# Sums over sought rows placed ahead of the last twelve tiles of a product

## The chip, the cores and the metric

The kernel runs on one NeuronCore of a Trainium2 chip. Five engines work on their own instruction streams and wait for one another only through semaphores: TensorE (PE, matmuls into PSUM; its weight loads are listed apart as PEld), VectorE (DVE), ScalarE (ACT), GpSimd (POOL) and SyncE (SP), which here only issues transfers. All transfers share 16 DMA engines; SP, ACT and POOL each have a queue into them. The metric is the device time of one execution in microseconds, and the kernel before takes 2162.47 us in the median of 6 runs (2161.07 to 2164.54).

## The reference

Three graph convolutions on 6250 nodes with 256 features and 200000 edges, sorted by their destination, and then a feed-forward layer on the half of the nodes with the highest weight:

```python
x = x + gnn(layernorm(x))                  # three of the following, relu after the first two
    # h = x @ W
    # agg = segment_sum(h[src] * dinv[src] * dinv[dst], dst) + own term;  agg + b
    # dinv = rsqrt(deg), deg = edges into the node, and one for itself
x = x + ffn(layernorm(x))
    # weights = x @ wr + br;  the top half less one are chosen
    # y = gelu(sel @ w1 + b1) @ w2 + b2, scaled by the weight, added at its place
```

The change is in the preparation for the first convolution: deg and dinv, the product of the normed x with W1, and the places in the sorted edge list at which each piece of work begins.

## The kernel before

The nodes are 49 tiles of 128 (`NT = 49`). Tiles 0 to 30, where most edges lead, are done by counts: a strip of a destination tile holds how many edges lead from each node to each of its 128 nodes, and the convolution is a dense product of strips with hl, the scaled x W1 of all nodes. The rest is done by messages: the rows of edges are gathered and added up. hl is 49 x 2 x 256 values in each partition: a value, and what rounding it left.

All engines but SP run in the order in which the program is written (the whole front is under a hand-made schedule), so the place of a call in the text is its place in each engine's queue.

**The front, in order.** x is loaded in 7 groups of 7 tiles (three buffers). For each group, `fetch_rows` gathers with 7 indirect DMAs (L340, POOL) one row of 200 destinations for each node of 7 tiles: the row in which the node's edges end. `spread_of` takes mean and variance (L361, DVE), `roots` and `scales` make of them the scale and offset of each row of x, and then for each tile:

- `normal(t)`: the normed tile c_z (L397, ACT), and its two transposes (L400, PE)
- `product(t - 1)`: the copy c_zt out of PSUM (L293, ACT), and four matmuls with W1 (L298, PE)
- `stored(t - 2)`: the copy of the product into raw (L409, ACT)
- `seek(t)`: how many destinations in the tile's row lie before the node's end (L349, DVE), into a column of c2

After the last tile come: spread (L438, DVE), upto (L441, DVE), the matmuls L443 and L444 (PE) that turn upto into first, the number of edges before each node (L447, DVE), and `begins`. There are 20 "columns", each a list of 128 places in the edge list from which 128 edges are read: columns 0 to 16 for the counts and 17 to 19 for the messages (`SD = 17`, `SC = 20`). `begins(a, b)` makes the places of columns a to b - 1: a matmul for each column (L456, PE; 128 x 128 weights, 8 columns moved, two instructions for a column), a sum on DVE (junk_s, L458), and three small operations for the whole call (L461 to L463), the last of which writes `at`. It is called for column 0, then dinv is made (deg, whole_deg, a root on ACT at L272, four refining operations on DVE), and then it is called for the 19 others. Four small checks follow ("fits": matmuls L473, c_over L475). They are the last readers of the front's buffers, whose space hl then takes.

**From there to the main loop.** `take(a)` gathers with two indirect DMAs (L764, POOL) the destinations and sources of column a's edges; two columns are under way at a time. `codes_of` makes codes of them (7 operations on DVE, or 3 for columns 17 to 19), `flipped` transposes them (L794, PE), and `column` copies them out of PSUM (L805 or L808 and L809, ACT). `send_x(i)` makes hl of 7 tiles of raw (L814 on ACT, L815 on DVE, seven of each, about 2.9 us) and sends them to `sent[0]` in HBM (L818, SP, 1792 KB), where the message gathers find them. `count_bank` fills a strip: one-hot rows of 12 groups of edges at a time (L669, DVE, made one batch ahead), matmuls of these (L689, PE), and a copy of each bank of PSUM into the strip (L705, ACT). The first strip, of tile 30, has 16 banks of two groups each. The order before is:

```python
    send_x(0); next_column(); flip(); next_step()
    send_x(1)
    next_column()
    for k, bank in enumerate(BANKS[first_tile]):
        s = count_bank(...)          # send_x(2), (3), (4), (5) after banks 1, 5, 9, 13
    counted(...)                     # the strip's diagonal on DVE, and its transfer
    send_x(6)
```

**The main loop** (layer 0) has 7 steps for each of the 31 tiles. A step casts a seventh of a strip into piece (L727 on ACT, in some steps L729 on DVE), does its 7 matmuls with hl (L735, PE), in the first five steps of a tile fills some banks of the next tile's strip (three a step for tile 29, of three groups each), and handles one more column: `flip()` for the last one read and `next_column()` for the one after, for as long as columns are wanted. From step 7 on it gathers messages (L600, POOL), four sets ahead; their sums (L632, PE) begin some steps later.

Of the kernel before, what the change touches and what calls it, by code (L numbers as in the profile page):

```python
# [9 lines left out]
FP = mybir.dt.float32  # L10
# [11 lines left out]
P = 128  # L22
# [85 lines left out]
def by_counts(  # L108
# [303 lines left out]

    for t in range(XG):
        spread_of(t)
    scaled = scales(0, *roots(0))
    for a in range(0, NT, XG):
# [5 lines left out]
        for t in range(a, a + XG):  # L422
            normal(t, *scaled)
            product(t - 1)
            stored(t - 2)
            seek(t, found[t - a])
            if t == a + 1 and a + 2 * XG < NT:
                xts[a + 2 * XG] = load_x(a + 2 * XG)
        if a + XG < NT:
            scaled = scales(a + XG, *root)  # L430
        if 0 < a <= 4 * XG:
            in_order(a // XG - 1)
    product(NT - 1)
    stored(NT - 2)
    stored(NT - 1)
# [12 lines left out]


    begin = f1p.tile([P, SC], FP, name="begin")  # L450

    def begins(a, b):
        for c in range(a, b):
            t0 = TILE0[c]
            ps_s = ps_f.tile([P, SPAN], FP, name="ps_f")
            nc.tensor.matmul(ps_s, spread[:, c * P : (c + 1) * P], first[:, t0 : t0 + SPAN], start=True, stop=True)  # L456
            junk = small.tile([P, SPAN], FP, name="junk_s")
            nc.vector.scalar_tensor_tensor(  # L458
                junk, ps_s, 1.0, plan_sb[:, 3:, c], op0=OP.mult, op1=OP.mult, accum_out=begin[:, c : c + 1]
            )  # L460
        nc.vector.tensor_add(begin[:, a:b], begin[:, a:b], plan_sb[:, 1, a:b])  # L461
        nc.vector.tensor_scalar(begin[:, a:b], begin[:, a:b], float(E), None, op0=OP.min)
        nc.vector.tensor_copy(at[:, a:b], begin[:, a:b])  # L463

    begins(0, 1)
    nc.vector.tensor_sub(deg, upto[:, 1:], first)
    whole_deg = f1p.tile([P, NT], FP, name="whole_deg")
    nc.vector.tensor_scalar(whole_deg, deg, 1.0, 1.0, op0=OP.add, op1=OP.max)
    rsqrt(dinv, whole_deg, NT)
    begins(1, SC)  # L470
    for i in range(len(WIDTHS)):
        ps_w = ps_f.tile([P, NT], FP, name="ps_f")
        nc.tensor.matmul(ps_w, fits_sb[:, i, :P], deg, start=True, stop=True)  # L473
        over = small.tile([P, NT], FP, name="c_over")
        nc.vector.tensor_tensor(over, ps_w, fits_sb[:, i, P:], op=OP.is_gt)  # L475
        nc.vector.tensor_reduce(bad[:, 2 + i : 3 + i], over, axis=AX.X, op=OP.add)
    front.close()
    gnn = ExitStack()
    hl_pool = gnn.enter_context(tc.tile_pool(name="gnn1", bufs=1, side="right"))

    hl = hl_pool.tile([P, NT, 2, D], FR, name="hl")


    lay = ExitStack()
    later = {}
    ps_a = lay.enter_context(tc.tile_pool(name="c_ps_a", bufs=2, space=PSUM))
# [23 lines left out]
    def finish():  # L510
        while behind:
            next_step()

# [245 lines left out]

    def take(a):  # L760
        got = {}
        for name in ("dst", "src"):
            got[name] = f3p.tile([P, P], I32, name=f"got_{name}")
            nc.gpsimd.indirect_dma_start(  # L764
                out=got[name], out_offset=None, in_=ends[name],
                in_offset=bass.IndirectOffsetOnAxis(ap=at[:, a : a + 1], axis=0),
            )
        return got

    def codes_of(a, got):  # L770
        base, width = plan_sb[:, 0, a : a + 1], plan_sb[:, 2, a : a + 1]
        both = f3p.tile([P, 2, P], FP, name="both", bufs=1)

        j1 = f3p.tile([P, P], FP, name="j1", bufs=1)
# [927 lines left out]
```

## Time and profile before

The profiled execution took 2166.06 us, its span is 2164.2 us (the rest lies around it).

| | us | place |
|---|---|---|
| loads and the first three groups | 0 to 56.9 | x, transfers of the edge list |
| the other groups, up to the last sought row | 56.9 to 88.9 | L349 ends at 88.9 |
| x's product ends | 97.2 | L298 |
| column 0's places, dinv | 97.9 to 101.1 | L456, L276 to L281 |
| the 19 other columns | 101.2 to 109.6 | L456 |
| fits | 108.6 to 111.3 | L473 to L476 |
| first hl to the first matmul of the main loop | 111.16 to 146.72 | L814 to L735 |
| layer 0 to 2, feed-forward | to 2164.2 | |

In the whole span PE is busy 89% of the time, DVE 63%, ACT 56%, POOL 59%. In the front these shares say little: which engine is waited for changes every few microseconds, and so the front is read by the chain of waits and by windows. A window's row gives busy time and number of instructions of PE, PEld, DVE, ACT and POOL, then the clock that TensorE was granted (1.00 is full speed), the share of the DMA engines and GB/s. A timeline row gives start, duration, engine, line and names, the number of instructions merged into it, and in brackets how long the engine had stood idle and what ended that.

### The profile page before, as it was taken

The numbers are of one execution on the slowest core, as the hardware profiler recorded it, in microseconds if no ns is written. First come the engines' busy times: TensorE is split into PE (matmuls) and PEld (weight loads), VectorE is DVE, ScalarE is ACT, GpSimd is POOL, SyncE is SP. The second block draws the span as 40 slices with busy tenths as digits, with TensorE's granted clock in tenths as the row PEclk, the third lists the DMA queues.
The fourth block names the chain that finished last, engine by engine and source line by source line (L and its number), as shares of the span: only waits on it lengthen the run. The fifth ranks groups of instructions, "written<-read, shape, count | busy, mean of one in ns | idle before, by whom it ended". The sixth has DMA issues, their size and how long they took to land.

```text
span 2164.2 us, 30448 instructions
## 1 busy us (share of the span) xinstructions
PE 1920.6 (89%) x9636; PEld 1468.0 (68%) x9636; DVE 1366.5 (63%) x3370; ACT 1209.0 (56%) x1986; POOL 1268.5 (59%) x1228
## 2 busy tenths in 40 slices
PE   4949999999989886799999999999999999928997
PEld 3726767677766665478888888767777777716665
DVE  6685555667667778365555555488888888862111
ACT  3777777766656642565555555576666666502111
POOL 5425776666766530377777777477777777602221
PEclk9959999999999999899999999999999999957999
DMA  7387787888877640787777777598888888612110
GB/s 204 96 291 221 234 261 237 259 247 245 261 226 211 198 132 24 233 267 224 215 215 214 212 213 217 155 298 254 257 251 262 255 256 257 206 58 61 59 47 18
DMA packets 229052, 435.60 MB, mean 201 GB/s; under 512 B 35358, under 2 KB 139092, under 8 KB 224881
## 3 DMA queue, kind: packets, MB, share of 16 engines
q0 software_dynamic: 92992, 205.70, 34.9%
q1 hardware_dynamic: 104357, 192.11, 27.6%
q10 hardware_dynamic: 31532, 35.75, 4.9%
q8 instruction: 78, 1.28, 0.2%
q14 instruction: 93, 0.76, 0.1%
HBM read 335.50 MB, written 99.61 MB: 201 GB/s over the span
## 4 chain that ended last, share of the span: by engine, by line
PE 60%; DVE 21%; DMA 8%; ACT 6%; issue 3%; POOL 1%; ACTq 0%; SPq 0%; DVEq 0%; POOLq 0%
PE c_pa L735 32%; PE ps_g L632 9%; PE c_ph L1135 4%; PE c_po L1143 4%; PE ps_b L689 4%; PE c_pt L298 4%; DVE half L624 3%; ACT strip L705 2%; DVE hot_l L669 2%; DVE hot_w L669 2%; DMA message<-sent 2%; DMA half<-sent,source 2%; DMA c_xt<-in_x 1%; DVE pick_sel L609 1%; ACT piece L727 1%
## 5 line engine op out<-in xcount | busy, mean ns | idle before, releaser
L735 PE MATMUL c_pa<-hl,piece 128*128 128x512 f32 x4557 | 1264.2, 409 | 28.2 <-DVE hl L952 15.2
L735 PEld LDWEIGHTS c_pa<-hl,piece 128*128 128x128 f32 x4557 | 831.7, 191 | 195.9 <-DVE hl L952 15.3
L600 POOL DMA_INDIRECT msg<-sent,source x718 | 731.2, 1018 | 357.3 <-issue 145.9
L600 POOL DMA_INDIRECT half<-sent,source x359 | 392.3, 1093 | 209.0 <-issue 73.5
L609 DVE TENSOR_TENSOR pick_sel<-up_h,local 128x256 fp32r<-128x256 f16 x540 | 227.3, 421 | 284.3 <-PE ps_g L632 282.8
L705 ACT ACTIVATE strip<-ps_b 128x441 f16<-128x441 f32 (+3 forms) x441 | 303.4, 754 | 149.6 <-PE ps_b L689 147.7
L632 PE MATMUL ps_g<-half,pick_sel 128*128 128x512 f32 x1077 | 347.6, 401 | 37.3 <-DVE half L624 30.9
L619 ACT ACTIVATE half<-msg 128x512 fp32r<-128x512 f32 x360 | 225.3, 626 | 231.8 <-PE ps_g L632 156.7
L727 ACT ACTIVATE piece<-whole 128x896 fp32r<-128x896 f16 x341 | 320.3, 942 | 55.0 <-PE c_pa L735 27.8
L624 DVE TENSOR_TENSOR half<-msg,half 128x512 fp32r<-128x512 f32 x360 | 248.2, 689 | 81.5 <-ACT half L619 79.2
L689 PE MATMUL ps_b<-hot_w,hot_l 128*128 128x98 f16 (+2 forms) x2171 | 212.9, 225 | 64.9 <-DVE hot_l L669 48.1
L632 PEld LDWEIGHTS ps_g<-half,pick_sel 128*128 128x128 f32 x1077 | 200.4, 189 | 98.0 <-DVE half L624 48.8
L689 PEld LDWEIGHTS <-hot_l 128*128 128x128 f16 x2171 | 136.7, 101 | 182.4 <-issue 112.5
L727 ACT ACTIVATE piece<-strip 128x896 fp32r<-128x896 f16 x159 | 150.8, 950 | 99.9 <-PE c_pa L735 89.2
L669 DVE TENSOR_TENSOR hot_w<-up_w,codes 128x1176 f16<-128x1176 f16 (+2 forms) x181 | 165.4, 914 | 43.7 <-PE ps_b L689 43.4
L669 DVE TENSOR_TENSOR hot_l<-up_l,codes 128x1536 f16<-128x1536 f16 x181 | 172.1, 951 | 0.0
L1139 ACT ACTIVATE ht<-c_ph,b_sb 128x512 f32<-128x512 f32 (+2 forms) x64 | 38.0, 594 | 188.7 <-PE c_ph L1135 188.7
L1151 POOL DMA_INDIRECT out<-o,pick x25 | 25.2, 1007 | 140.8 <-DVE o L1148 140.8
L1147 DVE TENSOR_TENSOR o<-c_po,b_sb 128x256 f32<-128x256 f32 x25 | 10.6, 424 | 149.2 <-PE c_po L1143 149.2
L298 PE MATMUL c_pt<-c_wg,c_zt 128*128 128x256 f32 x392 | 99.8, 379 | 0.5 <-ACT c_zt L293 0.5
L1135 PE MATMUL c_ph<-yt,w_sb 128*128 128x512 f32 (+2 forms) x256 | 91.1, 516 | 0.6 <-DVE yt L1130 0.6
L1143 PE MATMUL c_po<-w_sb,ht 128*128 128x256 f32 x400 | 88.9, 382 | 0.0
(218 smaller groups left out, 1546.8 us busy)
## 6 DMA issues: line engine op xcount, KB each, us to landing
whole<-counts SPq DMA_DIRECT2D x434, 224.0 KB
counts<-strip SPq DMA_DIRECT2D x31, 1568.0 KB
c_rows<-ys ACTq DMA_DIRECT2D x49, 256.5 KB
sent<-hl SPq DMA_DIRECT2D x7, 1792.0 KB
sent<-c_h ACTq DMA_DIRECT2D x98, 128.0 KB
message<-sent SPq DMA_DIRECT2D x98, 128.0 KB
msg<-sent,source POOLq DMA_INDIRECT x718
c_xt<-in_x SPq DMA_DIRECT2D x48, 128.0 KB
```

The source lines that it names most:

```text
L298: nc.tensor.matmul(pt[:, 1, :], zt[:, k, :], w_sb[:, k, :], start=(k == 0), stop=(k == KD - 1))
L600: nc.gpsimd.indirect_dma_start(out=out_j, out_offset=None, in_=sent[layer], in_offset=bass.IndirectOffsetOnAxis(ap=source[:, i : i + 1], a ...
L609: nc.vector.tensor_tensor(pick[:, :n], up_h[:, None, :].to_broadcast([P, n, P]), local[:, b * GB : b * GB + n, None].to_broadcast([P, n, P ...
L619: nc.scalar.activation(half[:, :n, 0, :], msg[:, :n], AF.Copy)
L624: nc.vector.tensor_sub(half[:, :n, 1, :], msg[:, :n], half[:, :n, 0, :].bitcast(FP))
L632: nc.tensor.matmul(open_sums[t], pick[:, j, :], half[:, j].rearrange("p two d -> p (two d)"), start=(k == 0), stop=False)
L669: nc.vector.tensor_tensor(rows_k[:, : n // 2, :cols, :], up[:, None, :cols, :].to_broadcast([P, n // 2, cols, 2]), code.rearrange("p (k tw ...
L689: nc.tensor.matmul(pb[:, at_c : at_c + NT * width], row_l[:, k // 2, :, k % 2], row_w[:, k // 2, : NT * width, k % 2], start=(c == 0), sto ...
L705: nc.scalar.activation(strip[:, :, d0 : d0 + n * width].rearrange("p h (a j) -> p a h j", j=width), pb[:, at_c : at_c + n * NT * width].re ...
L727: nc.scalar.activation(piece, counts_7, AF.Copy)
L735: nc.tensor.matmul(pa, piece[:, j, :], hl[:, q].rearrange("p two d -> p (two d)"), start=(i == sources[0] and j == 0), stop=(i == sources[ ...
L1135: nc.tensor.matmul(ph[:, : n * P], w1_sb[:, k, f * P : (f + 1) * P], yt[:, k, : n * P], start=(k == 0), stop=(k == KD - 1),)
```

## The change

The last twelve tiles of x's product (`PAUSE = NT - 12 = 37`, tiles 37 to 48) are taken out of the loop over groups, where only their rows are still sought. After the last row come spread, upto, first, column 0's places, column 0's two gathers, and dinv. Then the twelve tiles are done, and after each of them the places of two more columns (1 and 2 after the first, one alone after the tenth, none after the last two); after the sixth also column 0's codes on VectorE. Behind the last product come column 0's transposes, the fits, the gathers of columns 17 and 18, and column 0's copy. The sends of x are spread over the 16 banks of the first strip: send 0 ahead of bank 0, sends 1 to 6 ahead of banks 2, 4, 6, 9, 11 and 13, and none after the strip. Column 17 is no longer handled ahead of the main loop but in its first step, and each later column a step later than before. The functions `take`, `codes_of`, `flipped`, `column` and the small scheduler move up in the text unchanged.

```diff
+    PAUSE = NT - 12
+
+    def x_product(t):
+        normal(t, *scaled[t // XG])
+        product(t - 1)
+        stored(t - 2)
+
     for t in range(XG):
         spread_of(t)
-    scaled = scales(0, *roots(0))
+    scaled = {0: scales(0, *roots(0))}
...
         for t in range(a, a + XG):
-            normal(t, *scaled)
-            product(t - 1)
-            stored(t - 2)
+            if t < PAUSE:
+                x_product(t)
             seek(t, found[t - a])
...
         if a + XG < NT:
-            scaled = scales(a + XG, *root)
+            scaled[a // XG + 1] = scales(a + XG, *root)
         if 0 < a <= 4 * XG:
             in_order(a // XG - 1)
-    product(NT - 1)
-    stored(NT - 2)
-    stored(NT - 1)
...
     begins(0, 1)
+    early_column = take(0)
     nc.vector.tensor_sub(deg, upto[:, 1:], first)
...
     rsqrt(dinv, whole_deg, NT)
-    begins(1, SC)
+    step_c = 2
+    for k, t in enumerate(range(PAUSE, NT)):
+        x_product(t)
+        if 1 + k * step_c < SC:
+            begins(1 + k * step_c, min(SC, 1 + (k + 1) * step_c))
+        if k == 5:
+            early_both = codes_of(0, early_column)
+    assert 1 + (NT - PAUSE) * step_c >= SC
+    product(NT - 1)
+    stored(NT - 2)
+    stored(NT - 1)
+    flipped(0, early_both)
     for i in range(len(WIDTHS)):
...
     columns_by = [0] + list(range(SD, SC)) + list(range(1, SD))
-    taken = [(columns_by[0], take(columns_by[0])), (columns_by[1], take(columns_by[1]))]
-    last_take = 2
+    taken = [(a, take(a)) for a in columns_by[1:3]]
+    last_take = 3
...
     first_tile = TILES_BY[0]
-    send_x(0)
-    next_column()
-    flip()
     next_step()
-    send_x(1)
     strips[first_tile] = f3p.tile([P, NT, P], F16, name="strip", bufs=1)
-    next_column()
+    sends = NT // XG
+    n_banks = len(BANKS[first_tile])
     for k, bank in enumerate(BANKS[first_tile]):
+        for i in range(ceil(sends * k / n_banks), ceil(sends * (k + 1) / n_banks)):
+            send_x(i)
         s = count_bank(strips[first_tile], first_tile, bank, s)
-        if k % 4 == 1 and k // 4 + 2 < NT // XG:
-            send_x(k // 4 + 2)
     counted(strips[first_tile], first_tile)
-    for k in range(2 + (len(BANKS[first_tile]) + 2) // 4, NT // XG):
-        send_x(k)
     raws.close()
```

## The prediction

> **What bounds the kernel now.** The change touches only the start, up to the main loop's first steps, so I read the start alone. First the chain of waits, which says what the start is made of:
>
> ```profile
> 78.12 0.32 DVE c_bn L361
> 79.00 0.60 ACT c_z L397
> ...
> 95.44 1.73 PE ps_x L298 x8
> ...
> 101.25 7.50 PE ps_f L456 x34
> ...
> 111.16 0.52 ACT hl L814
> ```
>
> From 79.0 to 97.2 us the chain runs over the last 14 tiles of x's product (TensorE and ScalarE in lockstep, 16.5 us from the first c_z to the last c_zt, 1.18 us a tile), then a short serial piece, then the 19 column sums (L456), four fit sums (L473), and only then does ScalarE begin hl. Next VectorE's timeline, for the moment from which the sums could start:
>
> ```profile
> 88.49 0.42 DVE L349 TENSOR_SCALAR_CACHE_REDUCE junk_r<-row,after_f 128x200 bf16<-128x200 uint16 x1
> 88.84 1.55 DVE L438 TENSOR_SCALAR spread<-row_sb,node_f 128x2560 f32<-128x2560 f16 x1
> 90.31 0.21 DVE L441 SCALAR_TENSOR_TENSOR upto<-c,c 128x49 f32<-128x49 f32 x1
> 97.59 0.21 DVE L447 COPY first<-ps_f 128x49 f32<-128x49 f32 x1 [7.07 <-PE ps_f L444]
> ```
>
> The sought rows end at 88.9 because their gathers land then (VectorE waits for row in front of four of the last six); VectorE has upto at 90.5 and waits 7.07 us behind x's product. That wait is what the change takes away. ScalarE's timeline shows the second place:
>
> ```profile
> 117.32 0.38 ACT L805 ACTIVATE codes<-ps_b 128x256 f16<-128x256 f32 x1 [3.26 <-PE ps_b L794]
> 117.60 2.89 ACT L814 ACTIVATE hl<-raw,c_dinv 128x256 fp32r<-128x256 f32 x7
> 124.36 0.89 ACT L705 ACTIVATE strip<-ps_b 128x392 f16<-128x392 f32 x2 [3.87 <-PE ps_b L689]
> ```
>
> ScalarE idles 3.26 and 3.87 us for the first column's codes and the first one-hot rows; from 124.36 on it is full until the loop. Last the windows, cut where the granted clock can change (its changes here all lie on a grid of 3.41 us); after the bounds come TensorE, its weight loads, VectorE, ScalarE, GpSimd, then the clock:
>
> ```profile
> 45.97:49.39 3.42, 0.00 (x0) 0.00 (x0) 3.21 (x13) 0.00 (x0) 0.00 (x0) 1.00 0.67 203
> 49.39:52.80 3.41, 1.65 (x5) 1.47 (x6) 3.31 (x20) 2.00 (x6) 1.53 (x2) 0.50 0.81 203
> 52.80:56.21 3.41, 3.41 (x11) 2.66 (x11) 2.11 (x9) 1.63 (x5) 2.50 (x4) 0.50 0.55 176
> ...
> 104.00:107.41 3.41, 3.41 (x17) 3.41 (x17) 1.39 (x16) 0.00 (x0) 0.00 (x0) 0.50 0.00 0
> ...
> 820.80:824.21 3.41, 3.02 (x23) 2.19 (x22) 2.27 (x3) 0.61 (x1) 0.00 (x0) 0.50 0.00 0
> 824.21:827.62 3.41, 1.47 (x28) 1.17 (x26) 3.40 (x5) 0.00 (x0) 0.00 (x0) 1.00 0.00 0
> 1960.85:1964.26 3.41, 2.61 (x12) 2.42 (x12) 0.85 (x2) 0.55 (x2) 2.51 (x3) 0.50 0.76 203
> 1964.26:1967.68 3.42, 2.83 (x13) 2.42 (x13) 0.42 (x1) 0.55 (x2) 1.89 (x2) 0.50 0.74 211
> ```
>
> An idle window halves the clock for the next one. A full window of x's product (52.80) restores it, but a window of nothing but column sums (104.00), busy throughout, does not. So I count the time in which columns move: at half clock 0.213 us for a transpose and 0.427 for a product matmul (an x tile is 2 and 4 of them, 2.13 us, as 51.15 to 53.34 to 55.48 us in the timeline), but 0.013 for a column sum of 8 columns, though these start 0.213 apart for their weight loads. By that count 1960.85 (12 of 0.213 us) has 0.75 and stays half; 820.80 has 0.77 (three of 0.427, about seventeen of 0.082) and the clock returns. Downwards, windows with 0.38 or less lose it, 0.39 keeps it.
>
> **The change, part by part.** *Removed:* the 7.07 us wait. *Lost:* TensorE and ScalarE did some seven of the twelve tiles while rows were still coming and upto was made (1.18 us each). Now both stand idle from 82.0 (the end of tile 35's product) to 90.6: 8.6 us hold a whole idle window wherever the grid lies, so TensorE restarts at half clock.
>
> *Serial piece.* Before, from L443's start at 97.01 to at (99.03) 2.0 us; at half clock four loads and two columns cost some 0.6 more, so at is ready near 93.2. deg, whole_deg and the root take from 98.95 to 99.65 before, so 93.9; c_z then reaches TensorE 0.64 later: 94.5.
>
> *Twelve tiles and 19 columns on TensorE.* Two columns add four loads: at half clock 3.5 spacings of 0.213 = 0.75 us (a transpose's load is about half a column's: 183 against 288 ns), so a step is 2.88; at full clock loads start 0.11 apart (97.85 to 98.21), so 0.36 and a step 1.54. ScalarE needs 1.08 a tile, VectorE about 1.1 a step for two junk_s and three small operations: both are covered. codes_of(0) at step 5, seven operations of 2.0 us, is covered by VectorE's slack, and without it would cost up to 2. Moved time in a window of these steps: 0.65 to 0.80 of it, above 0.77 for more than half of the positions. I take a return of the clock 6.5 us after the start (one to two windows, 3.4 at best, 12 after three bad ones). Then 6.5/2.88 = 2.26 tiles are done at half clock; 9.74 x 1.18 + 7.25 x 0.36 = 14.1 us follow, 0.9 for the last product: 94.5 + 6.5 + 14.1 + 0.9 = 116.0. The flip of column 0 (0.25) and four fits with their c_over, 0.43 each on VectorE, end 2.0 later: hl starts at 118.0 against 111.16, **+6.8 us**. Each window of 3.41 us more at half clock costs 1.6.
>
> [...]
>
> *From hl to the loop.* Before: first c_pa 35.56 us after hl's start (111.16 to 146.72). Now the codes are there: after send 0 (2.9), VectorE's tail (0.5), one-hot rows (2.2) and the first sums (0.6) the first strip comes at 6.1 us, after one idle time of 3.2 instead of 3.26 + 3.87. That is 3.9 less on ScalarE, which then does the same 16 strips and 6 sends without a break; column 17's flip, 0.5 us of ScalarE, moves from the first loop step to a later one where it is covered by matmuls. Against it: the rows for the next tile (2.0 us, VectorE) now lie after the last send and ahead of the strip's diagonal, so c_pa itself starts only 3.1 earlier. Bounds 2.4 and 5.4 (7.1 if both idle times vanished); the first steps' chain runs over ScalarE's strips and pieces, so I take **-4.0**.
>
> *Queues.* SP: seven sends of 1792 KB, issued 114.65 to 145.99 before, now closer together; at some 380 GB/s each needs 4.8 us, and they end several us earlier after hl's start. Nothing is gained: the first message gather (162.30) follows directly on the column gathers of GpSimd's queue. GpSimd: column 0's two gathers (0.94 each) start near 93.5 and have 8 us to land; the later columns' come one step later, the last before step 7's messages, whose sums begin at 186 in the profile: some 13 us of cover for some 4 us. *Downstream* nothing else moves.
>
> Sum: +6.8 - 4.0 = +2.8 us. The profiled execution took 2166.06 us (span 2164.2), 3.6 above the median of 2162.47; I set the difference on the median: **2165.3**.
>
> **The rivals.** *1. The clock does not return among the columns.* For it: 0.75 was not enough, and 0.80 is my own count. Then 12 x 2.13 + 9 x 0.75 + 0.37 + 1.7 - 0.8 (a late return) = 33.6, hl at 94.5 + 33.6 + 2.0 = 130.1, +18.9 - 4.0 = +14.9: 2177.4. *2. Faster.* TensorE keeps full clock through the gap and both idle times of ScalarE vanish: start 93.7, 12 x 1.18 + 9.5 x 0.36 + 0.9 = 18.5, hl at 114.2, +3.0 - 7.7 = -4.7: 2157.8. It decides from where the second stage gives more than the first costs; the idle window at 45.97 speaks against the first half, the one-hot rows against the second. *3. The change does not overlap:* columns and product alternate with stalls through the two ps_f banks, 0.3 us a step, 10 steps: 2168.3. VectorE's slack speaks against it.
>
> **How the numbers follow.** Likeliest 0.60, rival 1 0.27, rival 2 0.06, rival 3 0.07. The likeliest one's own range: return at 3.4 us (-1.4) with -5.4, to 12 us (+2.6) with -2.4: 2162.5 to 2169.5. The whole range drops most of rival 2 and keeps rival 1: 2161.5 to 2178.5. About 0.2%, 4.3 us, is what a measurement can tell from no change: two thirds of the likeliest case (0.40) lie within it; its rest (0.20), rival 1 and rival 3 lie above (0.54), rival 2 below (0.06).
>
> **What would show it.** first (L447) near 91.5 with no wait on L444; no TensorE work from 82 to 90.6; half clock at 94.5, full from about 101; hl at 118; no wait of ScalarE for codes, one of about 3 us for the first strip; c_pa about 32 us after hl. A clock still half at 110 means rival 1; hl before 114 rival 2. I am wrong if the loop's first steps give back what ScalarE gained, or if the restart at half clock does not happen.

## The result and the profile after

The changed kernel takes 2171.59 us in the median of 25 runs (2161.96 to 2176.53), the kernel before beside it on the same chip 2162.78 us (50 runs): a ratio of 1.0034, 95% interval 1.0026 to 1.0042, or +7.4 us (5.6 to 9.1). A second comparison of the same pair gave 1.0022 (1.0010 to 1.0034), +4.8 us. The ratios are taken over all fast runs (one run of the kernel before, of 4855 us, is slow and left out) and not from the medians, which lie 8.8 and 2.9 us apart. The change makes the kernel slower, as forecast and by more than forecast. The profiled execution took 2170.12 us, its span is 2168.2 us; its sought rows end at 86.88 us instead of 88.92, a difference that no edit explains, so the stages below are counted from the end of the rows.

Line numbers have moved: spread is L441, upto L444, first L450, the column sums L537, a column's gathers L483 and its codes L494 to L506, hl L830 and L831, the strip's copies L773, its diagonal L789, piece L795 and L797, the loop's matmuls L803.

First TensorE's timeline of the changed kernel (start, duration, line, names; in brackets the idle time before and what ended it). It answers the wait of 7.07 us shown for before:

```profile
79.68 0.38 PE L298 MATMUL ps_x<-c_wg,c_zt 128*128 128x256 f32 x1
88.53 0.66 PE L446 MATMUL ps_f<-upto,up 128*128 128x49 f32 x2 [8.47 <-DVE upto L444]
...
92.46 0.69 PE L400 MATMUL ps_x<-c_ident,c_z 128*128 128x128 f32 x2 [1.94 <-ACT c_z L397]
95.36 0.67 PE L400 MATMUL ps_x<-c_ident,c_z 128*128 128x128 f32 x2
97.78 0.42 PE L400 MATMUL ps_x<-c_ident,c_z 128*128 128x128 f32 x2
99.27 0.42 PE L400 MATMUL ps_x<-c_ident,c_z 128*128 128x128 f32 x2
100.75 0.41 PE L400 MATMUL ps_x<-c_ident,c_z 128*128 128x128 f32 x2
```

The wait behind x's product is gone: TensorE now waits 8.47 us for upto. The first step of the twelve, transposes to transposes, takes 2.90 us; from 97.78 on a step takes 1.48 us. Two different speeds for the same work are the clock, which the windows show (us; busy time and number of PE, PEld, DVE, ACT, POOL; clock; DMA share; GB/s):

```profile
80.20:83.61 3.41, 0.00 (x0) 0.00 (x0) 1.63 (x9) 0.00 (x0) 2.52 (x3) 1.00 0.30 90
83.61:87.03 3.42, 0.00 (x0) 0.00 (x0) 1.44 (x7) 0.00 (x0) 0.95 (x1) 0.51 0.22 60
87.03:90.44 3.41, 1.61 (x6) 1.43 (x6) 1.65 (x4) 0.00 (x0) 0.00 (x0) 0.50 0.00 0
90.44:93.85 3.41, 1.47 (x6) 1.22 (x6) 2.24 (x12) 2.04 (x6) 1.88 (x2) 0.50 0.09 19
93.85:97.27 3.42, 3.42 (x13) 2.97 (x12) 0.85 (x7) 1.26 (x3) 0.00 (x0) 0.50 0.08 19
97.27:100.68 3.41, 3.41 (x26) 3.18 (x25) 1.69 (x14) 2.38 (x7) 0.00 (x0) 1.00 0.00 0
```

One idle window, 80.20 to 83.61, halves the clock from 83.6 on; the first full window of the steps, 93.85 to 97.27, brings it back. ScalarE's timeline shows the second stage:

```profile
113.47 0.38 ACT L524 ACTIVATE codes<-c_pt 128x256 f16<-128x256 f32 x1
114.94 2.90 ACT L830 ACTIVATE hl<-raw,c_dinv 128x256 fp32r<-128x256 f32 x7 [1.09 <-DVE c_over L569]
121.18 0.89 ACT L773 ACTIVATE strip<-ps_b 128x392 f16<-128x392 f32 x2 [3.34 <-PE ps_b L757]
121.95 2.90 ACT L830 ACTIVATE hl<-raw,c_dinv 128x256 fp32r<-128x256 f32 x7
```

The two idle times of before, 3.26 and 3.87 us, have become one of 3.34. The loop's first matmul starts at 146.42, 31.47 us after hl (35.56 before). Up to here the forecast holds. Then come the loop's first steps, for which it had expected no change; VectorE's timeline there:

```profile
159.16 0.23 DVE L501 TENSOR_SCALAR hi_i<-got_src 128x128 int32<-128x128 int32 x1 [1.27 <-DMA got_src<-src_p,at]
...
164.46 0.28 DVE L494 TENSOR_SCALAR j<-got_dst,plan_sb 128x128 f32<-128x128 int32 x1 [1.57 <-DMA got_dst<-dst_p,at]
164.92 0.23 DVE L501 TENSOR_SCALAR hi_i<-got_src 128x128 int32<-128x128 int32 x1 [0.17 <-DMA got_src<-src_p,at]
...
166.71 0.22 DVE L789 TENSOR_TENSOR strip<-strip,c_ident_h 128x128 f16<-128x128 f16 x1
166.84 0.62 DVE L797 CAST piece<-strip 128x896 fp32r<-128x896 f16 x1
```

VectorE does its work here in the order of the program: it waits for the gathered edges of columns 1 and 2, and behind these waits stand the strip's diagonal and a piece for the loop. TensorE's next matmuls wait for the diagonal:

```profile
166.93 0.41 PE L513 MATMUL ps_b<-c_ident,both 128*128 128x128 f32 x2 [2.34 <-DVE strip L789]
```

The chain of waits of this stretch agrees; its longest piece is that gather:

```profile
154.69 0.29 DVE j L494
...
156.50 8.33 DMA got_src<-src_p,at
...
166.24 0.24 DVE hi_i L505
```

So between loop steps 4 and 5 the changed kernel loses 2.9 us: counted from the first matmul of the loop, steps 4, 5 and 7 start after 15.17, 20.68 and 24.15 us, before after 15.62, 18.19 and 21.57.

### The profile page after: what moved, and what is told of

Its sections match the earlier page's. It is cut to its first block, busy times and chain, and to the rows that moved or that the text cites. A ratio compares the mean times of both kernels' runs of the same rounds, so it can differ in the third digit from the quotient of the medians.

```text
span 2168.2 us, 30475 instructions
## 1 busy us (share of the span) xinstructions
PE 1911.6 (88%) x9636; PEld 1459.6 (67%) x9636; DVE 1371.7 (63%) x3397; ACT 1210.3 (56%) x1986; POOL 1276.1 (59%) x1228
## 3 DMA queue, kind: packets, MB, share of 16 engines
q1 hardware_dynamic: 104357, 192.11, 27.5%
## 4 chain that ended last, share of the span: by engine, by line
PE 60%; DVE 21%; DMA 9%; ACT 5%; issue 3%; POOL 1%; ACTq 0%; SPq 0%; DVEq 0%; POOLq 0%
PE c_pa L803 33%; PE ps_g L700 9%; PE c_po L1154 4%; PE c_ph L1146 4%; PE ps_b L757 4%; PE c_pt L298 4%; DVE half L692 2%; DVE hot_w L737 2%; DVE hot_l L737 2%; DMA msg<-sent,source 2%; DMA c_xt<-in_x 2%; ACT strip L773 2%; DVE pick_sel L677 1%; DMA half<-sent,source 1%; DVE c_z L596 1%
## 5 line engine op out<-in xcount | busy, mean ns | idle before, releaser
L803 PE MATMUL c_pa<-hl,piece 128*128 128x512 f32 x4557 | 1263.4, 409 | 29.7 <-DVE hl L963 14.8
L803 PEld LDWEIGHTS c_pa<-hl,piece 128*128 128x128 f32 x4557 | 830.2, 191 | 198.9 <-DVE hl L963 17.7
L773 ACT ACTIVATE strip<-ps_b 128x441 f16<-128x441 f32 (+3 forms) x441 | 303.9, 754 | 146.2 <-PE ps_b L757 143.9
L795 ACT ACTIVATE piece<-whole 128x896 fp32r<-128x896 f16 x341 | 320.1, 942 | 59.2 <-PE c_pa L803 30.2
L795 ACT ACTIVATE piece<-strip 128x896 fp32r<-128x896 f16 x159 | 150.7, 950 | 99.5 <-PE c_pa L803 88.9
```

The costliest lines, as they stand in the source:

```text
L773: nc.scalar.activation(strip[:, :, d0 : d0 + n * width].rearrange("p h (a j) -> p a h j", j=width), pb[:, at_c : at_c + n * NT * width].re ...
L795: nc.scalar.activation(piece, counts_7, AF.Copy)
L803: nc.tensor.matmul(pa, piece[:, j, :], hl[:, q].rearrange("p two d -> p (two d)"), start=(i == sources[0] and j == 0), stop=(i == sources[ ...
```

## Where the time went, in all profiles

Each row is one profiled execution; the first column is counted from the end of the last sought row to the first hl, the second from there to the first matmul of the loop, the third from there to loop step 7. "Ahead" is the number of columns whose gathers are issued ahead of the loop. The kernels are explained below; the last two ran on a chip on which the kernel before, too, takes 2399 us.

| kernel | rows to hl | hl to loop | loop to step 7 | ahead | ratio to before |
|---|---|---|---|---|---|
| before | 22.2 | 35.6 | 21.6 | 4 | 1 |
| after | 28.1 | 31.5 | 24.2 | 3 | 1.0034 |
| after_again | 30.4 | 31.5 | 25.8 | 3 | 1.0022 |
| first_half | 27.9 | 32.0 | 21.5 | 4 | 1.0019 |
| second_half | 25.4 | 31.4 | 25.7 | 3 | 1.0018 |
| col17_ahead | 30.2 | 32.1 | 22.6 | 4 | 1.0023 |
| three_takes | 28.9 | 31.5 | 20.8 | 4 | 0.9999 |
| warm | 26.4 | 31.5 | 23.5 | 3 | 1.0003 |
| pause5 | 27.9 | 31.5 | 25.3 | 3 | 1.0014 |
| pause5_three | 27.6 | 31.5 | 20.6 | 4 | 0.9997 |
| pause5_three_warm | 21.5 | 31.5 | 20.6 | 4 | 0.9952 |
| late_sends | 28.3 | 31.5 | 23.8 | 3 | 1.0026 |
| before_extra | 27.5 | 35.6 | 21.5 | 4 | 0.9983 |
| after_extra | 29.0 | 31.5 | 25.5 | 3 | 0.9968 |

For the changed kernel the first profile gives +5.8 - 4.1 + 2.6 = +4.3 us, the second +8.2 - 4.1 + 4.2 = +8.3; the two measured differences are +7.4 and +4.8. The runs of one kernel on one chip scatter by 4 to 10 us to either side of their median, and some of that lies behind these stages: from step 7 to the end of the span it is 1997.6 us in the first profile of the changed kernel and 1991.4 in the second. So the sum of stages is good to a few microseconds and no more. The third column splits by the fourth without overlap: 20.6 to 22.6 us with four columns ahead, 23.5 to 25.8 with three.

The table below says why. It gives, for three columns, when their two gathers are issued and when VectorE first reads each of the two (columns are handled in the order 0, 17, 18, 19, 1, 2, and so on; times from the timelines of GpSimd and VectorE):

| column | issued before | read before | issued after | read after (wait) |
|---|---|---|---|---|
| 19 | 121.48, 122.72 | 150.35, 151.87 | 146.83, 148.08 | 154.69, 155.35 (0.38) |
| 1 | 147.09, 148.33 | 155.36, 155.56 | 150.24, 151.71 | 157.62, 159.16 (1.27) |
| 2 | 150.90, 152.37 | 159.26, 159.64 | 155.25, 156.50 | 164.46, 164.92 (1.57, 0.17) |

For column 2, GpSimd's issues and VectorE's first readers, before:

```profile
150.90 0.95 POOL L764 DMA_INDIRECT got_dst<-dst_p,at  x1 [1.63 <-DVE j L775]
152.37 0.94 POOL L764 DMA_INDIRECT got_src<-src_p,at  x1 [0.52 <-DVE both L778]
159.26 0.27 DVE L775 TENSOR_SCALAR j<-got_dst,plan_sb 128x128 f32<-128x128 int32 x1
159.64 0.23 DVE L782 TENSOR_SCALAR hi_i<-got_src 128x128 int32<-128x128 int32 x1
```

and its issues after (the readers are shown above, at 164.46 and 164.92):

```profile
155.25 0.95 POOL L483 DMA_INDIRECT got_dst<-dst_p,at  x1 [2.59 <-DVE j L494]
156.50 1.15 POOL L483 DMA_INDIRECT got_src<-src_p,at  x1 [0.30 <-issue]
```

Before, columns 0, 17, 18 and 19 are gathered ahead of the loop, and the loop's first steps handle 18, 19, 1 and 2. After, column 17 is one step later, the buffer of its gathers comes free one step later, and the loop's first steps must gather column 19 as well and handle five columns. Where VectorE waits, the time from issue to reading is the time that the gather takes, its landing and the signal of it included: 7.3 to 9.2 us, while the sends and the counts fill the DMA engines. Before, the two gathers of columns 1 and 2 are read 8.3 and 7.2 us after their issue, without a wait. After, VectorE stands in line for them after 7.4 to 7.6 us (157.62 - 150.24; it is done with the one-hot rows at 162.89, column 2's gather was issued at 155.25) and, for the second one, after 6.2 to 6.6: about 1 us sooner, and that is too soon.

## The experiments

The rival views were: the front alone costs the time and the rest is a gain; the waits in the loop are a chance of one execution; the gathers land late because of what fills the queue, or only when it is empty. The letters in the expectations name such views.

**col17_ahead**: the changed kernel, with column 17 handled ahead of the loop again, behind the sends of bank 0.

```diff
     for k, bank in enumerate(BANKS[first_tile]):
         for i in range(ceil(sends * k / n_banks), ceil(sends * (k + 1) / n_banks)):
             send_x(i)
+        if k == 0:
+            next_column()
```

> The changed kernel, with column 17 handled ahead of the first strip again (its codes after send 0, and the next gathers issued there), so that every later column comes in the step in which it came before the change. Theory A (a column a step later meets gathers that land late while the sends fill the DMA engines, and VectorE waits for it ahead of the strip's diagonal and the next piece): the 2.9 us that the changed kernel loses between its loop steps 4 and 5 (from -0.75 to +2.18 us against before) go, 0.6 us of VectorE ahead of the first one-hot rows come back: some 2.3 us less than the change, a ratio of 1.0024 instead of 1.0034. Theory B (all of the loss is the restart at half clock and the idle gap ahead of it, the loop only shifts noise): no difference from the change, 1.0034.

Measured: 2169.43 us against 2165.66, 1.0023 (1.0011 to 1.0035); the interval holds both figures. The loop's first steps came back to 22.6 us, but column 17's work now stands in ScalarE's stretch (hl to loop 32.1 instead of 31.5), and in the profiled execution the clock returned only 9.3 us after x's restart at 94.75. The repair works where it was aimed, and the total can't tell the two theories apart.

**three_takes**: the changed kernel, with a third pair of buffers for gathers, so that columns 17, 18 and 19 are gathered ahead of the loop.

```diff
-            got[name] = f3p.tile([P, P], I32, name=f"got_{name}")
+            got[name] = f3p.tile([P, P], I32, name=f"got_{name}", bufs=3)
...
-    taken = [(a, take(a)) for a in columns_by[1:3]]
-    last_take = 3
+    taken = [(a, take(a)) for a in columns_by[1:4]]
+    last_take = 4
```

> The changed kernel with three columns' gathers under way instead of two (three buffers each), the columns themselves in the order of the change. Theory A1 (the gathers of columns 1 and 2 land late, 8 to 9 us after issue, because sends fill the DMA engines): each gather is issued a loop step, some 3.5 us, earlier, so the wait of about 2.9 us at step 5 goes: 1.0021. Theory A2 (not the landing but the 2 us of codes on VectorE in step 4, in front of the diagonal): little changes, 1.0032 to 1.0036.

Measured: 2165.0 us, 0.9999 (0.9985 to 1.0013). Five columns are still handled in the first steps, but VectorE's timeline has no wait for them any more:

```profile
159.13 0.28 DVE L494 TENSOR_SCALAR j<-got_dst,plan_sb 128x128 f32<-128x128 int32 x1
159.32 0.22 DVE L501 TENSOR_SCALAR hi_i<-got_src 128x128 int32<-128x128 int32 x1
...
163.01 0.28 DVE L494 TENSOR_SCALAR j<-got_dst,plan_sb 128x128 f32<-128x128 int32 x1
163.21 0.22 DVE L501 TENSOR_SCALAR hi_i<-got_src 128x128 int32<-128x128 int32 x1
```

The first steps take 20.8 us, 0.8 less than before and 3.3 less than with the change. So it isn't the number of columns that costs the time, but the time from issue to need. The total lies 5 to 8 us below the changed kernel's two ratios, more than these 3.3 us and below both expected figures; what goes beyond the 3.3 us is not explained, and is within the scatter of the runs.

**warm**: the changed kernel, with idle matmuls on TensorE in the gap (nobody reads their result): 16 ahead of spread and 4 behind column 0's places.

```diff
+    def warm(n):
+        pt = ps_t.tile([P, 2, D], FP, name="c_pt")
+        for _ in range(n):
+            nc.tensor.matmul(pt[:, 1, :], ident, wg_sb[0][:, 0, :], start=True, stop=True)
+
+    warm(16)
...
     begins(0, 1)
+    warm(4)
```

> The changed kernel with 16 matmuls whose result nobody reads ahead of the matmuls that make first, and 4 more after column 0's sum, which keep TensorE moving through the time in which it idles. If the restart at half clock costs what the changed profile shows (from 92.46 to 97.30 us at half clock, 1.7 steps that take 2.5 us at full clock, and 0.6 us in the serial piece): 2.9 us less than the change, 1.0021. If the clock returns later in most executions than in the profiled one, more: up to 1.000. If the idle gap alone counts and not the clock: 1.0034.

Measured: 2167.1 us, 1.0003 (0.9987 to 1.0018). hl starts 26.4 us after the rows instead of 28.1, and the steps ran at full clock from 94.7 on, 0.2 us after the restart. So part of what the clock costs can be bought back: 1.7 us of hl's start in these two profiles, where 2.9 were expected. The total is lower than that accounts for, but its runs lie between 2156.69 and 2170.32 us.

**first_half**: the changed front with the order of before from hl on (send 0, send 1, one column, then the sends behind banks).

```diff
+    send_x(0)
+    send_x(1)
...
-    sends = NT // XG
-    n_banks = len(BANKS[first_tile])
+    next_column()
     for k, bank in enumerate(BANKS[first_tile]):
-        for i in range(ceil(sends * k / n_banks), ceil(sends * (k + 1) / n_banks)):
-            send_x(i)
         s = count_bank(strips[first_tile], first_tile, bank, s)
+        if k % 4 == 1 and k // 4 + 2 < NT // XG:
+            send_x(k // 4 + 2)
     counted(strips[first_tile], first_tile)
+    for k in range(2 + (len(BANKS[first_tile]) + 2) // 4, NT // XG):
+        send_x(k)
```

> The front of the change (sums ahead of the last twelve tiles, column 0's codes in their midst), but sends and column 17 in the order of before: sends 0 and 1 first, column 17's codes, then the strip with the others. First strip at 5.8 + 0.5 + 0.6 + 2.2 + 0.6 = 9.7 us after hl's start instead of 6.2, then 16 strips and 5 sends, so the first c_pa some 1.2 us later than in the change, and by theory A the 2.9 us of step 5 do not arise: 1.0026. By theory B it is 1.0040.

Measured: 2169.95 us, 1.0019 (1.0007 to 1.0031): the interval holds A's figure and not B's. One thing is worth keeping: hl to the loop is 32.0 us here, so 3.6 of the 4.1 us that the second stage gains come from the codes' being ready, and the spreading of the sends adds 0.5. And with column 17 ahead of the loop the first steps take 21.5 us, as before.

**second_half**: the front of before, column 0 made ahead of hl, and then the order of the change with its spread sends and column 17 in the loop.

```diff
     first_tile = TILES_BY[0]
-    send_x(0)
     next_column()
     flip()
     next_step()
-    send_x(1)
...
-    next_column()
...
+        for i in range(ceil(sends * k / n_banks), ceil(sends * (k + 1) / n_banks)):
+            send_x(i)
```

> The kernel before with only the second part of the change: its front as it was, then column 0's codes, flip and copy ahead of all sends, the sends spread over the banks as in the change, and column 17 a step later. hl starts some 3 us later (codes 2.0, flip 0.7, copy 0.4), the first c_pa 31.5 us after that: 0.9 us earlier than before. Theory A: step 5 then loses 2.9 us: +2.0 us, 1.0009. Theory B: -0.9 us, 0.9996.

Measured: 2167.34 us against 2162.97, 1.0018 (1.0003 to 1.0032), above both expectations, with A's figure inside the interval and B's outside. This half is no gain by itself: column 0 ahead of hl costs 3.1 us, hl to the loop gives 4.1, and the first steps lose 4.1 again, with the front of before. The loss in the loop belongs to the later columns, not to the change of the front.

**pause5** and **pause5_three**: five tiles instead of twelve are left behind the sums, with four columns a step, so that TensorE has no idle gap ahead of the sums; the second one with the third pair of buffers as well.

```diff
-    PAUSE = NT - 12
+    PAUSE = NT - 5
...
-    step_c = 2
+    step_c = 4
...
-        if k == 5:
+        if k == 3:
             early_both = codes_of(0, early_column)
```

> The changed kernel with the last five tiles after the sums instead of the last twelve (four columns after each tile, column 0's codes after the fourth). Seven tiles more are done while rows are still sought, which fills TensorE's idle 8.5 us almost up to upto. If the twelve tiles cost because seven of them had been free: x's part then takes 5 x 1.9 + 0.9 from about 94 us and, with a restart at half clock, 2.5 more; hl starts near 109 instead of 111.2, the second stage gives 4, the loop takes 2.9 back: -3.6 us, 0.9983. If the restart's cost were all: like the change, 1.0030.

> The same with three columns' gathers under way. Theory A1: 2.9 us less than with five tiles alone: -6.5 us, 0.9970. Theory A2: as that one, 0.9983.

Measured: 2167.18 us, 1.0014 (1.0000 to 1.0027), and 2163.76 us, 0.9997 (0.9984 to 1.0010). The third pair of buffers gives the loop's first steps 4.8 us (25.3 to 20.6), as A1 has it, but neither kernel is as fast as was expected. The gap was gone and the clock was still lost, and this time it didn't come back among the columns at all (half from 92.7 to 150.7 us, and from 92.3 to 150.3). The place is the short serial piece from first to c_z: in pause5_three's windows the stretch 88.91 to 92.33 holds 1.17 us of TensorE's work.

```profile
85.50:88.91 3.41, 3.32 (x19) 2.36 (x17) 2.14 (x7) 1.94 (x6) 0.00 (x0) 1.00 0.04 13
88.91:92.33 3.42, 1.17 (x8) 0.89 (x8) 2.08 (x12) 1.30 (x5) 1.10 (x2) 0.99 0.01 2
92.33:95.74 3.41, 3.41 (x14) 3.05 (x14) 1.06 (x10) 1.60 (x4) 0.78 (x1) 0.50 0.13 38
95.74:99.15 3.41, 3.41 (x15) 3.05 (x14) 1.03 (x9) 1.25 (x3) 0.00 (x0) 0.50 0.00 0
```

With four columns a step TensorE is busy throughout, and yet the clock stays at half: much of it is column sums, which move eight columns each (how much, is counted in the last section).

**after_again**: the changed kernel once more, for a second profile.

> The changed kernel once more, unaltered, beside the next kernels on their chip, and with a second profile. Both theories of the loop's first steps (A: VectorE waits in its queue for the gathers of column 2, which land 8 to 9 us after their issue while the sends fill the DMA engines; B: the waits of the first profile were a chance of that one execution) expect a ratio of 1.002 to 1.004. A expects in the second profile again a wait of more than 1 us of VectorE for got_src or got_dst between 158 and 166 us, and 2 to 3.5 us lost between the starts of loop steps 4 and 5 beside the kernel before; B expects neither.

Measured: 2170.11 us against 2167.23, 1.0022 (1.0010 to 1.0034). The waits are there again, in VectorE's timeline:

```profile
163.14 0.23 DVE L501 TENSOR_SCALAR hi_i<-got_src 128x128 int32<-128x128 int32 x1 [1.17 <-DMA got_src<-src_p,at]
...
167.99 0.29 DVE L494 TENSOR_SCALAR j<-got_dst,plan_sb 128x128 f32<-128x128 int32 x1 [1.12 <-DMA got_dst<-dst_p,at]
168.97 0.23 DVE L501 TENSOR_SCALAR hi_i<-got_src 128x128 int32<-128x128 int32 x1 [0.69 <-DMA got_src<-src_p,at]
```

Steps 4 and 5 start 15.1 and 20.7 us after the loop's start, as in the first profile: no chance. The clock was different. x restarts at 94.21, and the windows show three at half clock, the one of the restart included, before it returns at 103.8:

```profile
93.56:96.97 3.41, 2.76 (x10) 2.40 (x11) 1.39 (x7) 2.22 (x8) 1.64 (x2) 0.50 0.15 38
96.97:100.39 3.42, 3.42 (x14) 3.06 (x14) 1.11 (x12) 1.79 (x5) 0.00 (x0) 0.50 0.00 0
100.39:103.80 3.41, 3.41 (x14) 2.96 (x13) 1.31 (x10) 1.42 (x5) 0.00 (x0) 0.50 0.00 0
103.80:107.21 3.41, 3.41 (x24) 3.15 (x23) 1.70 (x15) 2.44 (x7) 0.00 (x0) 1.00 0.00 0
```

So the clock returns 9.6 us after the restart instead of 4.8, and hl starts 2.3 us later after the rows (1.6 for each window was the forecast's price). The kernel is the same; what differs is where the grid of windows lies.

**late_sends**: the transfers of sends 4 to 6 are issued in loop step 5; hl is made as before.

```diff
+        if i < 4:
+            send_out(i)
+
+    def send_out(i):
         nc.sync.dma_start(
...
+        if n == 5:
+            for k in range(4, NT // XG):
+                send_out(k)
```

> The changed kernel with the transfers of sends 4 to 6 issued in loop step 5 instead of as soon as their half of hl is made; ScalarE and VectorE make hl when they did. With that the DMA engines carry much less between 150 and 165 us. A (the gathers of column 2 land late because the sends fill the DMA engines) expects them to land 2 to 4 us after their issue, no wait of VectorE for got_src or got_dst above 0.3 us, and loop step 5 to start 2 to 3 us sooner after the first c_pa (18 to 18.5 us instead of 20.7). The rival (they land late for a reason that is not the load, or step 5 is late for another reason) expects 20 us or more. What the later transfers do to the first message gathers, which need all of hl, is left out of this: their land is some 7 us later, so the whole may be up to 7 us slower (1.002 to 1.006).

Measured: 2170.73 us, 1.0026 (1.0009 to 1.0044); step 5 starts 20.4 us after the loop's start, and VectorE waits 0.72 and 1.12 us for column 2. By the letter that is the rival's. But the edit didn't make what it was to make: SP runs ahead of the loop, and the last two transfers went out between 148.4 and 151.2 us, so the DMA engines' share stayed at 0.93 to 1.05 from 149 to 164 us. The run doesn't decide.

**after_extra** and **before_extra**: instead of taking load away, one transfer is added. Behind send 3 its bytes go a second time, to a spare place.

```diff
+    spare = dram.tile([7 * P, 2 * D], FR, name="spare")
...
     def send_x(i):
         ...
+        if i == 3:
+            nc.sync.dma_start(spare..., hl[:, i * XG : (i + 1) * XG]...)
```

> The changed kernel with one transfer more on SP's queue: behind send 3 its 1792 KB go a second time, to a spare place that nobody reads. The full stretch of the DMA engines, from the first send to the end of the last one and of the first counts (119.3 to 164.1 us in the changed kernel, 115.6 to 161.2 before, both 45 us), becomes some 4.9 us longer and ends 22.6 us after the first c_pa instead of 17.7. A1 (the gathers of column 2 land when that stretch ends, so its end is a floor for loop step 5) expects step 5 some 25.5 us after the first c_pa instead of 20.7, and the whole 1.004 to 1.006 against the kernel before. A2 (under load a gather takes some 8 us wherever in the stretch it is issued) expects step 5 at 20.5 to 21 us as without the transfer, and 1.002 to 1.004.

> The kernel before with the same second transfer. Its full stretch of the DMA engines ends 14.5 us after the first c_pa and would end at 19.4; the gathers that its loop needs earliest of that stretch are issued 4.2 and 5.6 us after the first c_pa and land at 10 to 12.5. A1 expects them to land at 17 to 19 us, so that loop steps 4 and 5 start 3 to 5 us later than the 15.6 and 18.2 us of the kernel before, and a ratio of 1.0015 to 1.0025. A2 expects steps 4 and 5 at 15.5 to 16 and 18 to 18.5 us and 1.000 to 1.001.

The chip of these two runs took 2399.2 us for the kernel before (2381.71 to 2420.39), so the ratios, 0.9968 (0.9936 to 0.9999) and 0.9983 (0.9950 to 1.0016), say little; hl to the loop is the same there as elsewhere (31.5 and 35.6 us), and only the loop's first steps are read. after_extra starts step 5 20.6 us after the loop's start (A1: 25.5, A2: 20.5 to 21), before_extra steps 4 and 5 after 15.5 and 18.1 (A1: 3 to 5 us later). A2 holds: the gathers don't wait for the end of the full stretch, but take some 8 us wherever in it they are issued. GpSimd's timeline of after_extra with the issues of column 2:

```profile
170.81 0.94 POOL L484 DMA_INDIRECT got_dst<-dst_p,at  x1 [2.31 <-DVE j L495]
172.08 1.65 POOL L484 DMA_INDIRECT got_src<-src_p,at  x1 [0.32 <-DVE both L498]
```

and VectorE's first readers of them, 8.2 and 8.7 us later:

```profile
179.04 0.29 DVE L495 TENSOR_SCALAR j<-got_dst,plan_sb 128x128 f32<-128x128 int32 x1 [1.32 <-DMA got_dst<-dst_p,at]
180.77 0.23 DVE L502 TENSOR_SCALAR hi_i<-got_src 128x128 int32<-128x128 int32 x1 [1.44 <-DMA got_src<-src_p,at]
```

No run takes the load away, so that it makes these 8 us is shown by comparison alone. Over the changed kernel's whole run, the view of the gathers of destinations gives a median of 3.0 us from issue to landing. (Its longest, 6.8, is the transfer's own landing where the view finds one; the figures above are read from the side of the waiting engine.)

```profile
DMA to landing us min/median/max: 2.4/3.0/6.8
```

The packets in the traces say more. A gather is 16 packets of 4 KB, and a trace gives the start and the end of each. In all 14 profiles (560 gathers) the transfers that GpSimd didn't issue kept the DMA engines busy for under a tenth of the first 1.6 us after the issue of 390 gathers, and for over 0.85 of it with 125. With the former the first packet starts 1.7 us after the issue and the last one ends after 2.4 (medians; a few reach 5.7 and 6.6), with the latter it is 5.4 and 6.1 us (2.7 to 6.4 and 3.4 to 7.7). So a gather's own transfer stays short, and what grows beside the sends is the time ahead of its first packet. Of the 9.2 us of column 2's first gather in the changed kernel, 6.4 lie ahead of its first packet, 0.8 are its packets, and 2.0 lie between its last packet and the end of VectorE's wait.

**pause5_three_warm**: what the runs pointed to, put together: five tiles, the third pair of buffers, and four idle matmuls in the serial piece.

```diff
     begins(0, 1)
+    warm(4)
     early_column = take(0)
```

(The cut shows what is new beside pause5_three; warm is the function shown above.)

> Only five tiles of x's product are left behind the column sums instead of twelve, three columns are taken ahead, and four idle matmuls (their result is read by nobody) stand on TensorE ahead of the restart, in the gap. If the granted clock stays at or returns to full by them: hl starts 17 us after the sought rows' end instead of 28.1 (before: 22.2), hl to c_pa 31.5, the loop 0.8 shorter than before: some 9 us faster than before, 0.9957, down to 0.997 if the clock stays half for one more window. Rival (the dummies do not hold the clock, as in the kernel without them where it stayed half from 92.7 to 150.7 us): hl 22 us after the rows' end and a ratio of 0.9985 to 1.000, as without them.

Measured: 2155.58 us against 2167.23, 0.9952 (0.9936 to 0.9969): 10.4 us faster than the kernel before (6.7 to 13.9). It beats both kernels. The clock stays at full speed through the serial piece and the columns:

```profile
86.24:89.66 3.42, 2.92 (x16) 1.94 (x15) 2.24 (x6) 1.39 (x4) 0.00 (x0) 1.00 0.00 0
89.66:93.07 3.41, 3.29 (x16) 2.59 (x17) 2.24 (x12) 1.89 (x6) 1.69 (x2) 1.00 0.09 22
93.07:96.48 3.41, 3.32 (x25) 3.01 (x24) 1.72 (x17) 2.27 (x6) 0.20 (x1) 1.00 0.09 19
...
99.90:103.31 3.41, 2.32 (x16) 2.03 (x16) 2.77 (x18) 1.07 (x3) 0.00 (x0) 1.00 0.02 5
103.31:106.72 3.41, 3.09 (x11) 2.63 (x11) 1.02 (x10) 0.51 (x2) 1.11 (x2) 0.50 0.00 0
```

The window 89.66 to 93.07 is the one that lost it in pause5_three; four matmuls make the difference (columns move in 0.78 of the window with them and in 0.14 without, counted as in the last section), 6.1 us of hl's start. But the expected total came with a wrong share: hl starts 21.5 us after the rows and not 17, because a step with four columns takes 2.14 us, column 0's codes hold TensorE up for 1.37 us, and the clock is lost again at 103.3, for the last product and the fits. By stages the version is worth -0.7 - 4.1 - 1.0 = -5.8 us at step 7. The two profiled executions are 10.4 us apart as well; the rest of that is 1.9 ahead of the end of the rows (87.03 against 88.92 us) and 2.8 behind step 7. The two profiles of the changed kernel alone differ by 1.7 and 6.2 us in these stretches (86.88 and 88.62; 1997.6 and 1991.4), so the rest can't be put down to the version; why its runs lie 6.7 us or more below the kernel before stays open.

## Why the prediction was right, and where it was wrong

The direction was right and the time is inside the range. The central figure is +2.8 us, measured were +7.4 and +4.8; by its ratio the first puts the kernel at 2169.8 us, just above the likeliest case's own range (up to 2169.5), and the median measured beside it, 2171.59 us, lies further above. That it is inside the whole range owes something to luck: the room up there was kept for rival 1, which did not come, and what filled it was a loss in the loop that the sum had put at nothing.

- *The serial piece and the gap* were right. Counted from the last row, VectorE makes first after 2.8 us (forecast 2.6), TensorE idles for 8.47 us (8.6), and it restarts at half clock.
- *The twelve tiles* were right. A step at half clock was put at 2.88 us and took 2.90, at full clock at 1.54 and took 1.48. The return of the clock was put 6.5 us after the restart, between 3.4 and 12. The six profiles with twelve tiles behind the front of the change and without idle matmuls, that of the last chip left out, show 4.4, 4.8, 5.3, 6.5, 9.3 and 9.6: a mean of 6.7, from which all but one lie more than 1 us away: the term was right on average, not for a single execution. hl was forecast 29.1 us after the rows; these six give 27.9 to 30.4, a mean of 28.9. VectorE's slack covers the codes but for some 0.5 us, the wait of TensorE for junk_s at 106.70 among it.
- *From hl to the loop* was right: one idle time of 3.34 us (3.2 forecast), 4.1 us saved (4.0).
- *Queues* is the step that failed, and with it the sentence on what lies downstream, that nothing else moves. It put the gathers of the later columns one step later at no cost, with "some 13 us of cover for some 4 us". The cover was measured to the sums of the messages; the first to wait for a column's gathers is VectorE's next codes_of, 6.2 to 7.6 us after their issue. And the 4 us were the author's estimate: beside free engines a gather's last packet ends 2.4 us after its issue (the median above); here a gather took 7.3 to 9.2. Both numbers could be read before: column 2's gathers, issued at 150.90 and 152.37, are read at 159.26 and 159.64 without any margin that the trace shows (the last packet of the second ends at 159.09), and the DMA engines' share from 149 to 158 us is 1.00 to 1.05. Nor do the sends end several us earlier after hl: by the packets the DMA engines are full, with gaps of 1 to 2.5 us, from 115.6 to 161.2 us before and from 119.3 to 164.1 after, which is until 50.0 and 49.2 us after hl, so the loop, which starts 4.1 us earlier after hl, meets more of them. The waits are 3.4 us in the first profile (0.38 + 1.27 + 1.57 + 0.17), the loop loses 2.6 us, 4.2 in the second.
- The sentence named as what would make it wrong, that the loop's first steps give back what ScalarE gained, is what happened, for two thirds of the gain or all of it.
- *Rival 1* (no return of the clock among the columns) was in none of the profiles of twelve tiles. It appeared where the steps held four columns, and there by the count of moved columns that the prediction used. *Rival 3* (stalls through the banks of ps_f) left one wait of 0.23 us with two columns a step, the one at 106.70 behind column 0's codes.
- *Smaller slips.* Rival 2 takes 7.7 us off for ScalarE's two idle times, which the step before had put at 7.1; its time would be 2158.4 us. The window at 820.80 has 0.79 of its time in moved columns, not 0.77, when all its twenty small matmuls are counted.

## What to carry to other kernels

When a step moves later in a ring of buffers, the next request into the ring moves with it: ask for each request how long after its issue the first reader stands in line for it, on the engine that takes its work in order, and set against that the landing time in that stretch (7.3 to 9.2 us here), not on free engines (2.4 us to the last packet). Where such a margin is near zero, try one more buffer (here one pair of 64 KB each): it took the waits away without moving any other work. And before idle time of TensorE is moved, look at how much is left in a window of the clock's grid (3.41 us here): four idle matmuls in a short serial piece were worth 6.1 us of hl's start, more than the 4.1 us that the change gained.

## What the runs showed of the hardware

The granted clock here is full or half (every record of it in the traces of before and after is 1.00 or 0.50), all its changes lie on a grid of 3.41 us, and it follows, as far as the count below can tell, the time in which columns move. Counted from each trace (0.213 us for a transpose and 0.427 for a product matmul of 256 columns at half clock, half of that at full clock, and a column sum by its 8 columns, each from the start that the trace gives), with its share of the window:

| window | share moved | without transposes | clock in it, and in the next |
|---|---|---|---|
| after_again, 97.0 | 0.75 | 0.52 | half, half |
| after_again, 100.4 | 0.80 | 0.66 | half, full |
| after, 1967.8 | 0.76 | 0.50 | half, full |
| after_again, 219.9 | 0.72 | 0.72 | half, half |
| three_takes, 147.6 | 0.78 | 0.78 | half, half |
| pause5_three, 95.7 to 109.3 | 0.57 to 0.70 | 0.52 to 0.58 | half, half |
| late_sends, 94.8 | 0.74 | 0.62 | half, full |
| after_extra, 107.5 | 0.76 | 0.52 | half, half |
| pause5, 700.3 | 0.37 | 0.19 | full, full |
| after_again, 216.5 | 0.36 | 0.36 | full, half |

The bounds aren't sharp by this count. Over all 14 traces a window returned the clock from 0.73 on (second_half, 891.3) and failed to with up to 0.78; one kept it from 0.36 on (after_again, 1885.6) and lost it with up to 0.41 (after_extra, 967.7). Without the transposes there is hardly any order: 0.50 and 0.62 would return the clock where 0.72 and 0.78 do not, and 0.19 would keep it where 0.36 loses it. So in these rows the transposes of this kernel count with the rest. Where the grid lies is not set by the restart: two executions of the same kernel got the clock back 4.8 and 9.6 us after the same restart, which came 1.39 us ahead of a boundary of the grid in the one (92.46 and 93.85) and 0.65 us behind one in the other (94.21 and 93.56).

That a profile calls TensorE busy says little about the clock: the windows from 95.74 to 112.81 in pause5_three are busy throughout and keep half clock.

The other surprise is the gathers: two of 64 KB each, issued while 1792 KB transfers fill the engines, took 7.3 to 9.2 us, most of it ahead of their first packets, and adding one more such transfer ahead of them didn't change that (7.3 to 8.7 in after_extra). And one chip took 2399 us for the kernel that took 2163 to 2167 on the others; the runs don't say why.
